# Gate statistics moved into the next image's gate, and the last stores of a group spread out

## The chip, the cores and the metric

The kernel runs on one core of one Trainium2 chip. The metric is the device time of the whole program in microseconds (us), the median of several executions. The core's engines are TensorE (PE), VectorE (DVE), ScalarE (ACT), GpSimd (POOL) and SyncE (SP), which here only issues transfers (DMAs). Each engine works through its own list of instructions in order; semaphores tie the lists together.

## The reference

The input x has 32 images of 8 channels of 256 x 256 numbers. Two layers follow one another, each added to its input; ahead of each stands a group normalisation over pairs of channels. Cut to what matters here:

```python
# layer 0, on the normalised x
grid = drive = x
for _ in range(15):                                   # the lattice
    mapped = 3.9 * grid * (1 - grid)
    physics = 0.7 * mapped + 0.3 * conv3x3_depthwise(mapped)
    grid = 0.85 * physics + 0.15 * drive
cml = clip(grid, 0.0001, 0.9999)
nca = sigmoid(conv1x1(relu(conv3x3(x, 8 -> 128)), 128 -> 8))
gin = concatenate([x, cml, nca])                      # 24 channels
g = sigmoid(conv1x1(relu(conv3x3(gin, 24 -> 8)), 8 -> 8))
y = x_in + g * cml + (1 - g) * nca
# layer 1: y normalised per image and pair of channels, quantised with
# sx = 127 / max(abs(normalised y)) over ALL images, 3x3 convolution
out = y + conv3x3(round(norm(y) * sx), round(w * sw)) / (sx * sw) + bias
```

So layer 1 needs, for each image, mean and variance of y (mean_y and rstd_y in the kernel), and the largest deviation over all images (dev_y), before it can start.

## The kernel before

**Two phases.** The first (up to about 13670 us) computes y for all 32 images and keeps it in scratch memory (y_s). The second quantises y, convolves it and writes the result. The change touches the first phase only.

**Four kinds of work in the first phase**, in groups of four images (GB = 4, NG = 8 groups):

- *prep* (normalise, L288): loads x, takes its statistics, writes normalised copies to scratch (xp_s, xq_s).
- *lattice* (L376): 8 channels of 15 steps for the four images of a group, as two streams of two images. A step goes over three tiles; for each tile and stream PE does matmuls (L486), DVE adds the drive (L494) and forms the next state (L499). Every second step neighbouring rows are exchanged by DMAs from m_a to m_a (exchange, L446). After the last step of a channel the result goes to scratch (cm_s) in 44 stores (store, L414).
- *nca* (L553): the hidden convolution (L563), the 1x1 convolution (L580), stores to nc_s.
- *gate* (L708): for each image ten iterations p over pairs of row blocks. An iteration loads nb from nc_s, cq from cm_s and xb from x (stage, L663, one iteration ahead), does three sets of convolution matmuls (L755, on xnb, cmb and nb), and then finishes the iteration before it (finish, L715: the 1x1 matmuls pg, sigmoid, mixing on POOL and DVE, bn_stats, maximum and minimum of the rows, a store to y_s).

**At an image's end** the gate forms the image's statistics from the rows' (L782 to L817): bn_aggr gives ma and mb, two matmuls add them up over the partitions (total, L785), DVE forms e from the mean, two more matmuls add up e, then come rstd_y and dev_y.

**Order of work.** PE's list is in the order in which the program is written out (manual_schedule, for PE alone); the lists of the other engines are put in order by a scheduler. The order of writing comes from generators: each `yield` gives the cost, in estimated us of PE, of what was written since the last. `together` (L823) writes a lattice step (5.91) and then as much filler as keeps filler and lattice in proportion; `both` (L837) mixes two fillers in proportion. While the lattice of group g is written, the filler is nca of group g, gate of group g-1 and prep of group g+1. For the last group the gates come alone, after everything else (L875).

**Background transfers.** The stores of a channel and the loads of the next channel's drive go into a list, `later`. After every lattice tile three of them are issued (background, L442). Only the last tile of a group's last channel issues all that is left at once, since the gate of that group, whose loads read cm_s, is written from the next lattice step on, and the store of a tensor has to be written out before the load that reads it.

Of the kernel before, what the change touches and what calls it, by code (L numbers as in the profile page):

```python
# [31 lines left out]
F32 = mybir.dt.float32  # L32
# [81 lines left out]
def kernel(  # L114
# [142 lines left out]
    with ExitStack() as one:  # L257
# [118 lines left out]
        def lattice(g):  # L376
# [65 lines left out]
            def background(n):  # L442
                for _ in range(min(n, len(later))):
                    nc.sync.dma_start(*later.pop(0))

            def exchange(t, k):  # L446

# [11 lines left out]
            for c in range(C):  # L459
                u = g * C + c  # L460
                ds = units[u]
                for step in range(STEPS):
                    if step == 7 and u + 1 < NG * C:
                        units[u + 1], dmas = load(u + 1)
                        later.extend(dmas)
                    if step == STEPS - 1:
                        background(len(later))
                    for i, ts in enumerate(tiles):

                        jobs = []  # L470
                        for s in range(2):
                            a2b = (step + s) % 2 == 0
                            n = NJ + 1 if a2b else NJ
                            pt = ps_c.tile([P, 512], F32, name="pt", tag="pt")
                            jobs.append((s, a2b, n, pt[:, : 6 * n].rearrange("p (t j) -> p t j", j=n)))

                        for part in range(3):
                            for s, a2b, n, pt in jobs:  # L480
                                own = m_a[s][:, ts, 1 : 2 + NJ] if a2b else m_b[s][:, ts, 0:NJ]
                                beside = m_a[s][:, ts, 0 : 1 + NJ] if a2b else m_b[s][:, ts, 1 : 1 + NJ]
                                low = a2b == (part != 1)
                                half = slice(0, 64) if low else slice(64, P)
                                k = 2 if part == 2 else 0 if a2b else 1
                                T.matmul(  # L486
                                    pt[half], lw[:, c, k, half], beside if part == 2 else own,
                                    start=part < 2, stop=part > 0,
                                )
                        for s, a2b, n, pt in jobs:  # L490
                            gt = gp.tile([P, 6 * (NJ + 1)], F32, name="gt", tag="gt")
                            gt = gt[:, : 6 * n].rearrange("p (t j) -> p t j", j=n)
                            d = ds[s][1 if a2b else 0]
                            V.scalar_tensor_tensor(gt, pt, FLOOR, d[:, ts, :], ALU.max, ALU.add)  # L494
                            if step == STEPS - 1:
                                V.tensor_scalar(d[:, ts, :], gt, 0.0001, 1.0 - 0.0001, ALU.max, ALU.min)
                                continue
                            to = m_b[s][:, ts, :] if a2b else m_a[s][:, ts, 1 : 1 + NJ]
                            V.scalar_tensor_tensor(to, gt, 1.0, gt, ALU.subtract, ALU.mult)  # L499
                            if a2b:  # L500

                                edge = m_b[s][:, ts, 0 : NJ + 1 : NJ]
                                G.tensor_tensor(  # L503
                                    edge, edge, junk.unsqueeze(1).to_broadcast([P, 6, 2]), ALU.mult
                                )
                        for s, a2b, n, pt in jobs:
                            for k in range(2):
                                if i != k + 1:
                                    continue
                                if step == STEPS - 1:  # L510
                                    b = g * GB + 2 * s + k
                                    later.extend(store(b, c, "b" if a2b else "a", ds[s][1 if a2b else 0], k))
                                elif not a2b:
                                    exchange(m_a[s], k)
                        if step == STEPS - 1 and u + 1 in units:
                            begin(units[u + 1], ts)

                        background(len(later) if (c, step, i) == (C - 1, STEPS - 1, 2) else 3)
                    yield 5.91

        ROWS = ((2, 4, 10, 12, 3, 5, 11, 13), (1, 6, 8, 14, 7, 9))
        FIRST, LAST = (2, 4, 10, 12), (1, 7, 9, 14)
# [185 lines left out]
        def gate(b):  # L708
# [37 lines left out]
            for p in range(10):  # L746
                n = 2 if p < 9 else 1
                xnb, xb, cmb, nb = ahead
                pa = ps_a.tile([P, 512], F32, name="pa", tag="acc")
                three = pa[:, : n * W].rearrange("p (k w) -> p k w", w=W)  # L750
                i = 0
                for s, t in ((0, xnb), (1, cmb), (2, nb)):
                    for dx in range(3):
                        for half in (slice(0, 64), slice(64, P)):
                            T.matmul(  # L755
                                three[half], gw[:, s * 3 + dx, half], t[:, :n, dx : dx + W],
                                start=(i == 0), stop=(i == 8),
                            )
                        i += 1
                    if s == 0 and p < 9:  # L760
                        ahead = stage(b, p + 1, sc)
                    elif s == 0 and (b + 1) % GB:
                        staged[b + 1] = begin_gate(b + 1)
                    if s < 2:
                        yield 2.6
                r1 = wk.tile([P, 512], F32, name="r1", tag="r1")
                S.activation(r1[:, : n * W], pa[:, : n * W], AF.Relu, bias=bv[:, 0:1])  # L767
                if last:
                    if done:
                        nc.sync.dma_start(*done)  # L770
                    done = finish(*last)
                yield 3.5
                last = (p, r1, xb, cmb, nb)
            if done:
# [2 lines left out]
            yield 0.9  # L777


            ma = st.tile([P, 2], F32, name="ma", tag="ma")  # L780
            mb = st.tile([P, 2], F32, name="mb", tag="mb")
            V.bn_aggr(ma, st_a.rearrange("p k s -> p (k s)"))  # L782
            V.bn_aggr(mb, st_b)

            def total(a, c):  # L785
                pm = ps_c.tile([P, 512], F32, name="pm", tag="pt")
# [1 line left out]
                T.matmul(pm[:, 0:1], sel_b, c, start=False, stop=True)  # L788
                return pm[:, 0:1]

            m, rstd = mean_y[:, b : b + 1], rstd_y[:, b : b + 1]
            yield 0.5
            V.tensor_copy(m, total(ma[:, 0:1], mb[:, 0:1]))
            e = st.tile([P, 2], F32, name="e2", tag="e2")
            for i, t in enumerate((ma, mb)):
                V.tensor_tensor(e[:, i : i + 1], t[:, 0:1], m, ALU.subtract)
                V.tensor_tensor(e[:, i : i + 1], e[:, i : i + 1], e[:, i : i + 1], ALU.mult)
                V.tensor_tensor(e[:, i : i + 1], e[:, i : i + 1], t[:, 1:2], ALU.add)
            yield 0.5
            V.tensor_scalar(rstd, total(e[:, 0:1], e[:, 1:2]), GN_EPS, None, ALU.add)  # L800
            G.tensor_tensor(rstd, rstd, mhalf[:, 0:1], ALU.pow)
            d = st.tile([P, 6], F32, name="dv", tag="dv")
            V.tensor_reduce(d[:, 0:1], mx[:, 0:9], AX.X, ALU.max)
            V.tensor_reduce(d[:, 1:2], mn[:, 0:9], AX.X, ALU.min)
            V.tensor_copy(d[:, 2:3], mx[:, 9:10])
            V.tensor_copy(d[:, 3:4], mn[:, 9:10])
            V.tensor_scalar(d[:, 0:4], d[:, 0:4], m, None, ALU.subtract)
            for i in range(2):
                V.tensor_scalar(
                    d[:, 2 * i + 1 : 2 * i + 2], d[:, 2 * i + 1 : 2 * i + 2], -1.0, None, ALU.mult  # L810
                )
                V.tensor_tensor(
                    d[:, 4 + i : 5 + i], d[:, 2 * i : 2 * i + 1], d[:, 2 * i + 1 : 2 * i + 2], ALU.max
                )
                V.tensor_tensor(d[:, 4 + i : 5 + i], d[:, 4 + i : 5 + i], masks[:, i : i + 1], ALU.mult)
            V.tensor_tensor(d[:, 4:5], d[:, 4:5], d[:, 5:6], ALU.max)
            V.tensor_tensor(dev_y[:, b : b + 1], d[:, 4:5], rstd, ALU.mult)  # L817

        def chain(*gens):
            for gen in gens:  # L820
# [38 lines left out]
            for b in range(g * GB, g * GB + GB):  # L859
                yield from f(b)  # L860

        units, later = {}, []
        T_NCA, T_GATE, T_PREP, T_LATTICE = 520.0, 340.0, 34.0, 8 * 45 * 1.97
        for _ in prep(0, (0,)):
            pass
        for g in range(NG):
            fill, t = images(nca, g), T_NCA
            if g:
                fill, t = both(fill, t, images(gate, g - 1), T_GATE), t + T_GATE
            if g + 1 < NG:  # L870
                fill, t = both(fill, t, prep(g + 1, (0, 1)), T_PREP), t + T_PREP
            if g == 0:
# [1 line left out]
            together(lattice(g), T_LATTICE, fill, t)  # L874
        for _ in images(gate, NG - 1):  # L875
            pass


    with ExitStack() as two:
# [110 lines left out]
```

## Time and profile before

| | |
|---|---|
| median of 3 runs | 14468.11 us (14463.03 to 14472.73) |
| profiled execution, span | 14446.0 us |
| mean granted TensorE clock | 0.959 |
| instructions | 229162 |
| groups | group 0 up to about 1670 us, then seven of some 1650 us; gates alone from 13257 to 13670 us; second phase to the end |

The page gives busy time for each engine. A row of a wait table names the engine and line that waited, the tile, what ended the wait, total us, number of waits and the longest. A timeline row has start, length, engine, line, operation, shapes, count, and in brackets how long the engine had been idle before it and what ended that. A row of a table by stretches gives, for a stretch of time, its length, the busy us of PE, PE's weight loads, DVE, ACT and POOL (with counts), the granted clock of TensorE (1.00 is full), the share of the DMA engines and GB/s. A float32 matmul counts as two passes, hence even counts.

### The profile page before, as it was taken

Reading aid. Unit: us, or ns where it says so; the run is one execution under the profiler, and the core shown is the slowest. Engines: PE = TensorE matmul, PEld = TensorE weight load, DVE = VectorE, ACT = ScalarE, POOL = GpSimd, SP = SyncE. Lnnn points to the kernel's source line nnn. Section 1 sums busy time; section 2 is a strip of 40 time slices with the busy share of each in tenths; the row PEclk is TensorE's granted clock in tenths of the full one; section 3 lists DMA queues with packets and bytes.
Section 4 is the critical chain, followed back from the end, with each engine's and each line's share of the span. In section 5 each row is a group of like instructions: output and inputs, shape, how many; then the busy total and the mean of one; then the engine's idle time right before and its main releaser. Section 6 shows DMA issues by size and latency. Waiting matters only on the chain.

```text
span 14446.0 us, 229162 instructions
## 1 busy us (share of the span) xinstructions
PE 13241.2 (92%) x81728; PEld 6420.6 (44%) x81728; DVE 8161.7 (56%) x16290; ACT 4043.5 (28%) x6274; POOL 2458.8 (17%) x4266
## 2 busy tenths in 40 slices
PE   2999999999999999999999999999999999999733
PEld 1554444444444444444444444444444444444211
DVE  3555555555555555555555555555555555555576
ACT  1333223232322232222223222322232222222122
POOL 1110111111111111111111111111111111112300
PEclk9999999999999999999999999999999999999866
DMA  5444444444444444444344434444444433333365
GB/s 149 93 101 93 92 99 105 101 95 104 105 97 101 106 98 98 101 100 111 88 101 105 108 91 102 103 108 94 97 104 108 95 84 80 86 75 79 114 195 176
DMA packets 2259557, 1496.71 MB, mean 104 GB/s; under 512 B 1061248, under 2 KB 2229504, under 8 KB 2258304
## 3 DMA queue, kind: packets, MB, share of 16 engines
q1 hardware_dynamic: 2176976, 1401.95, 41.1%
q10 hardware_dynamic: 81456, 80.12, 1.7%
q8 instruction: 663, 10.86, 0.3%
q14 instruction: 462, 3.78, 0.1%
HBM read 866.48 MB, written 478.69 MB: 93 GB/s over the span
## 4 chain that ended last, share of the span: by engine, by line
PE 76%; DVE 7%; DMA 7%; SPq 4%; issue 3%; ACT 1%; POOL 1%; ACTq 1%; POOLq 0%; DVEq 0%
PE pt L486 34%; PE ph L563 19%; PE pa L755 13%; PE acc L580 7%; DVE gt L494 2%; PE pg L721 1%; DMA im<-xp_s 1%; DMA out_dram<-ob 1%; SPq L941 1%; PE pt L934 1%; DVE m_b L499 1%; DMA yb<-y_s 1%; DMA m_a<-m_a 1%; DMA xb<-in_x_dram 1%; DMA xr<-in_x_dram 1%
## 5 line engine op out<-in xcount | busy, mean ns | idle before, releaser
L486 PE MATMUL pt<-m_a,lw 128*64 128x390 f32 x17280 | 5857.6, 497 | 160.4 <-DMA m_a<-m_a 121.4
L486 PE MATMUL pt<-m_b,lw 128*64 128x384 f32 x17280 | 5825.7, 492 | 23.0 <-DVE m_b L410 17.8
L573 ACT ACTIVATE h<-ph,bp_sb 128x512 f32<-128x512 f32 x4096 | 2584.7, 685 | 6258.0 <-PE ph L563 6187.8
L486 PEld LDWEIGHTS pt<-m_a,lw 128*64 128x64 f32 x17280 | 2312.1, 138 | 1824.9 <-issue 1670.8
L486 PEld LDWEIGHTS pt<-m_b,lw 128*64 128x64 f32 x17280 | 2316.1, 138 | 1601.4 <-issue 1465.6
L563 PE MATMUL ph<-im,wp_hi 48*128 48x512 f32 x12288 | 2713.5, 416 | 104.8 <-DMA im<-xp_s 54.4
L494 DVE SCALAR_TENSOR_TENSOR gt<-pt,d_b 128x390 f32<-128x390 f32 x2880 | 1610.6, 559 | 1828.2 <-PE pt L486 1824.9
L494 DVE SCALAR_TENSOR_TENSOR gt<-pt,d_a 128x384 f32<-128x384 f32 x2880 | 1584.9, 550 | 1826.9 <-PE pt L486 1826.5
L563 PE MATMUL ph<-im,wp_lo 48*128 48x512 f32 x12288 | 2598.5, 399 | 0.0
L503 POOL TENSOR_TENSOR m_b<-m_b,junk 128x12 f32<-128x12 f32 x2688 | 809.2, 301 | 8089.7 <-DVE m_b L499 7597.8
L563 PEld LDWEIGHTS ph<-im,wp_hi 48*128 48x128 f32 x12288 | 1331.4, 188 | 1013.5 <-DVE m_b L499 197.8
L499 DVE SCALAR_TENSOR_TENSOR m_b<-gt 128x390 f32<-128x390 f32 x2688 | 1562.5, 581 | 42.5 <-DVE gt L494 0.9
L499 DVE SCALAR_TENSOR_TENSOR m_a<-gt 128x384 f32<-128x384 f32 x2688 | 1525.9, 568 | 15.6
L563 PEld LDWEIGHTS ph<-im,wp_lo 48*128 48x128 f32 x12288 | 1327.1, 188 | 215.2
L580 PE MATMUL acc<-h,wu_z 128*32 128x512 f32 x8320 | 1170.7, 605 | 12.9 <-ACT h L573 7.3
L755 PE MATMUL pa<-xnb,gw 128*64 128x512 f32 (+1 forms) x3840 | 890.5, 596 | 0.2
L755 PE MATMUL pa<-cmb,gw 128*64 128x512 f32 (+1 forms) x3840 | 852.0, 576 | 10.0 <-POOL cmb L677 10.0
L755 PE MATMUL pa<-nb,gw 128*64 128x512 f32 (+1 forms) x3840 | 849.5, 574 | 0.0
L726 POOL TENSOR_TENSOR d<-cmb,nb 128x512 f32<-128x512 f32 x320 | 511.4, 1598 | 1608.5 <-DVE gate L730 1449.6
L730 DVE TENSOR_TENSOR gate<-gate,d 128x512 f32<-128x512 f32 x320 | 216.0, 675 | 870.3 <-ACT gate L723 856.3
L934 PE MATMUL pt<-qt,qw 128*128 128x512 bf16 (+1 forms) x960 | 269.2, 451 | 477.9 <-ACT ob L935 427.1
L767 ACT ACTIVATE r<-pa,bv 128x512 f32<-128x512 f32 x320 | 213.1, 666 | 1651.3 <-PE pa L755 1650.3
(132 smaller groups left out, 6966.1 us busy)
## 6 DMA issues: line engine op xcount, KB each, us to landing
im<-xp_s SPq DMA_DIRECT2D x1152, 193.5 KB
im<-xp_s SPq DMA_DIRECT2D x1216, 96.8 KB
d_a<-xq_s SPq DMA_DIRECT2D x2048, 36.0 KB
nb<-nc_s SPq DMA_DIRECT2D x288, 256.0 KB
cq<-cm_s SPq DMA_DIRECT2D x288, 256.0 KB
yb<-y_s ACTq DMA_DIRECT2D x29, 2432.0 KB
xb<-in_x_dram SPq DMA_DIRECT2D x544, 128.0 KB
xp_s<-hi SPq DMA_DIRECT2D x256, 258.0 KB
```

The lines of the kernel that those rows point to most:

```text
L486: T.matmul(pt[half], lw[:, c, k, half], beside if part == 2 else own, start=part < 2, stop=part > 0,)
L494: V.scalar_tensor_tensor(gt, pt, FLOOR, d[:, ts, :], ALU.max, ALU.add)
L499: V.scalar_tensor_tensor(to, gt, 1.0, gt, ALU.subtract, ALU.mult)
L503: G.tensor_tensor(edge, edge, junk.unsqueeze(1).to_broadcast([P, 6, 2]), ALU.mult)
L563: T.matmul(ph[:, :n].rearrange("p (h w) -> p h w", w=W), w[64 * i : 64 * i + 48, dx, :], rhs[:, :, dx : dx + W], start=(dx == 0 and w is w ...
L573: S.activation(h[:, :n], ph[:, :n], AF.Relu, bias=bp_sb)
L580: T.matmul(acc[32 * g : 32 * g + 32, :cols], wu_z[:, 24 - 8 * i : 56 - 8 * i], h, start=first, stop=last,)
L726: G.tensor_tensor(three(d), cmb[:, :n, 1 : 1 + W], nin, ALU.subtract)
L730: V.tensor_tensor(y[:, :cols], gt[:, :cols], d[:, :cols], ALU.mult)
L755: T.matmul(three[half], gw[:, s * 3 + dx, half], t[:, :n, dx : dx + W], start=(i == 0), stop=(i == 8),)
L767: S.activation(r1[:, : n * W], pa[:, : n * W], AF.Relu, bias=bv[:, 0:1])
L934: T.matmul(pt, qw[:, dx, :], q[:, k0 : k0 + n, dx : dx + W], start=(dx == 0), stop=(dx == 2))
```

## The change

There are two edits.

**Statistics in pieces.** What the end of an image's gate did in one go becomes three functions, put into a list `sums`: gather (the two bn_aggr), means (the first two matmuls and e), deviations (the other two matmuls, rstd_y, dev_y). Each iteration of the following image's gate takes one from the list, after finish of the iteration before; the last image's are run after the last gate. The two yields of 0.5 between the pieces go. The aim is that matmuls which need a result of DVE are not written directly behind the work that they wait for.

**The last stores of a group.** The burst goes, and the stores left over from a group's last channel are issued three after each tile in the first steps of the next group's lattice. A counter `issued` counts what was issued from the list, `stored[g]` is its value at which all stores of group g are out, and `after` holds back the gate of group g until then, handing out empty units of 4.0. The last group, with no lattice after it, still issues all at once. The aim is that SyncE is not taken up by a burst while the next group's lattice begins.

```diff
             def background(n):
                 for _ in range(min(n, len(later))):
                     nc.sync.dma_start(*later.pop(0))
+                    issued[0] += 1
...
-                        background(len(later) if (c, step, i) == (C - 1, STEPS - 1, 2) else 3)
+                        background(3)
                     yield 5.91
+
+            stored[g] = issued[0] + len(later)
+            if g == NG - 1:
+                background(len(later))
...
                     done = finish(*last)
+                if sums:
+                    sums.pop(0)()
                 yield 3.5
...
-            V.bn_aggr(ma, st_a.rearrange("p k s -> p (k s)"))
-            V.bn_aggr(mb, st_b)
...
-            yield 0.5
-            V.tensor_copy(m, total(ma[:, 0:1], mb[:, 0:1]))
...
-            yield 0.5
-            V.tensor_scalar(rstd, total(e[:, 0:1], e[:, 1:2]), GN_EPS, None, ALU.add)
...
+            def gather():
+                V.bn_aggr(ma, st_a.rearrange("p k s -> p (k s)"))
+                V.bn_aggr(mb, st_b)
+
+            def means():
+                V.tensor_copy(m, total(ma[:, 0:1], mb[:, 0:1]))
...
+            def deviations():
+                V.tensor_scalar(rstd, total(e[:, 0:1], e[:, 1:2]), GN_EPS, None, ALU.add)
...
+            sums.extend((gather, means, deviations))
...
+        def after(g, gen):
+
+            while issued[0] < stored[g]:
+                yield 4.0
+            yield from gen
...
             if g:
-                fill, t = both(fill, t, images(gate, g - 1), T_GATE), t + T_GATE
+                fill, t = both(fill, t, after(g - 1, images(gate, g - 1)), T_GATE), t + T_GATE
...
         for _ in images(gate, NG - 1):
             pass
+        while sums:
+            sums.pop(0)()
```

More of the change, by code (lines that the diff above doesn't have):

```diff
@@ L781, in gate @@
             mb = st.tile([P, 2], F32, name="mb", tag="mb")
-            V.bn_aggr(ma, st_a.rearrange("p k s -> p (k s)"))
-            V.bn_aggr(mb, st_b)
+            e = st.tile([P, 2], F32, name="e2", tag="e2")
+            m, rstd = mean_y[:, b : b + 1], rstd_y[:, b : b + 1]
             def total(a, c):
@@ L789, in total @@
                 return pm[:, 0:1]
-            m, rstd = mean_y[:, b : b + 1], rstd_y[:, b : b + 1]
-            yield 0.5
-            V.tensor_copy(m, total(ma[:, 0:1], mb[:, 0:1]))
[L794 to L798, printed above, removed]
@@ L799, in gate @@
-            yield 0.5
-            V.tensor_scalar(rstd, total(e[:, 0:1], e[:, 1:2]), GN_EPS, None, ALU.add)
[L801 to L816, printed above, removed]
@@ L817, in gate @@
-            V.tensor_tensor(dev_y[:, b : b + 1], d[:, 4:5], rstd, ALU.mult)
+            def gather():
[3 more added lines that the diff above has]
+                V.tensor_copy(m, total(ma[:, 0:1], mb[:, 0:1]))
+                for i, t in enumerate((ma, mb)):
+                    V.tensor_tensor(e[:, i : i + 1], t[:, 0:1], m, ALU.subtract)
+                    V.tensor_tensor(e[:, i : i + 1], e[:, i : i + 1], e[:, i : i + 1], ALU.mult)
+                    V.tensor_tensor(e[:, i : i + 1], e[:, i : i + 1], t[:, 1:2], ALU.add)
@@ new lines, in deviations @@
+            def deviations():
+                V.tensor_scalar(rstd, total(e[:, 0:1], e[:, 1:2]), GN_EPS, None, ALU.add)
+                G.tensor_tensor(rstd, rstd, mhalf[:, 0:1], ALU.pow)
+                d = st.tile([P, 6], F32, name="dv", tag="dv")
+                V.tensor_reduce(d[:, 0:1], mx[:, 0:9], AX.X, ALU.max)
+                V.tensor_reduce(d[:, 1:2], mn[:, 0:9], AX.X, ALU.min)
+                V.tensor_copy(d[:, 2:3], mx[:, 9:10])
+                V.tensor_copy(d[:, 3:4], mn[:, 9:10])
+                V.tensor_scalar(d[:, 0:4], d[:, 0:4], m, None, ALU.subtract)
+                for i in range(2):
+                    lo_, hi_ = d[:, 2 * i + 1 : 2 * i + 2], d[:, 2 * i : 2 * i + 1]
+                    V.tensor_scalar(lo_, lo_, -1.0, None, ALU.mult)
+                    V.tensor_tensor(d[:, 4 + i : 5 + i], hi_, lo_, ALU.max)
+                    V.tensor_tensor(
+                        d[:, 4 + i : 5 + i], d[:, 4 + i : 5 + i], masks[:, i : i + 1], ALU.mult
+                    )
+                V.tensor_tensor(d[:, 4:5], d[:, 4:5], d[:, 5:6], ALU.max)
+                V.tensor_tensor(dev_y[:, b : b + 1], d[:, 4:5], rstd, ALU.mult)
@@ L860, in images @@
                 yield from f(b)
-        units, later = {}, []
+        units, later, issued, stored, sums = {}, [], [0], {}, []
+        def after(g, gen):
+            while issued[0] < stored[g]:
+                yield 4.0
+            yield from gen
         T_NCA, T_GATE, T_PREP, T_LATTICE = 520.0, 340.0, 34.0, 8 * 45 * 1.97
```

## The prediction

> **What bounds the kernel now.** I read the page first (engine shares, the 40 slices), then TensorE's waits by line, then its timeline at one image's end, then stretches of time side by side.
>
> ```profile
> PE 13241.2 (92%) x81728; PEld 6420.6 (44%) x81728; DVE 8161.7 (56%) x16290; ACT 4043.5 (28%) x6274; POOL 2458.8 (17%) x4266
> ```
>
> PE's waits, the statistics with the largest other one (total us, times, longest):
>
> ```profile
> PE pt L486 <- DMA m_a<-m_a: 121.4, 41, 10.1
> PE pm L788 <- DVE dv L805: 88.4, 20, 4.6
> PE pm L787 <- DVE ma L782: 78.0, 11, 11.4
> PE pm L787 <- DVE dv L812: 23.5, 21, 1.5
> PE pm L788 <- DVE mb L783: 7.6, 12, 3.4
> PE pm L787 <- DVE e L798: 4.2, 4, 1.1
> ```
>
> TensorE (PE) bounds everything up to about 13670 us; the last 770 us (the second convolution, L934) are not touched. Five of the six are waits of four tiny 128x1 matmuls, the statistics of a finished gate image (L787, L788): 88.4 + 78.0 + 23.5 + 7.6 + 4.2 = 201.7 us. By stretches, 150.1 us of them lie between 1500 and 13257 us, in 27 images (5.6 us each), the rest in the tail, where only gates run. PE executes in program order, so lattice and NCA matmuls stand behind these four. One image's end in the interior, then one in the tail (start, length, idle before):
>
> ```profile
> 2109.49 0.38 PE L787 MATMUL pm<-ma,sel_a 128*128 128x1 f32 x2
> 2114.43 0.59 PE L788 MATMUL pm<-mb,sel_b 128*128 128x1 f32 x2 [4.56 <-DVE dv L805]
> 2116.03 0.56 PE L787 MATMUL pm<-e,sel_a 128*128 128x1 f32 x2 [1.01 <-DVE dv L812]
> 2116.94 4.58 PE L755 MATMUL pa<-xnb,gw 128*64 128x512 f32 x12
> ...
> 13364.58 1.46 PE L721 MATMUL pg<-r,gw 128*64 128x512 f32 x8
> 13377.44 0.58 PE L787 MATMUL pm<-ma,sel_a 128*128 128x1 f32 x2 [11.41 <-DVE ma L782]
> 13381.09 4.50 PE L755 MATMUL pa<-xnb,gw 128*64 128x512 f32 x12
> 13385.43 2.74 PE L755 MATMUL pa<-cmb,gw 128*64 128x512 f32 x12
> ```
>
> Twelve gate passes take 2.74 us normally, but 4.58 and 4.50 right after the pause: a pause costs another 1.8 us. The stretches (PE busy, PEld, DVE, ACT, POOL, then granted clock) say the same:
>
> ```profile
> 2100.00:2150.00 50.00, 44.43 (x271) 21.16 (x270) 26.05 (x69) 10.55 (x18) 6.24 (x14) 0.93 0.32 78
> 2150.00:2200.00 50.00, 50.00 (x326) 23.32 (x322) 28.33 (x59) 13.42 (x21) 8.46 (x16) 1.00 0.41 87
> ...
> 700.00:1500.00 800.00, 759.68 (x4954) 399.16 (x4952) 442.72 (x914) 256.33 (x402) 82.01 (x204) 0.96 0.44 97
> 3380.00:3740.00 360.00, 358.71 (x2268) 168.95 (x2266) 204.37 (x416) 107.04 (x164) 65.50 (x114) 1.00 0.41 100
> ```
>
> The first row holds an image's end, the second none. The third is group 0, which has no gate to fill with; the fourth has lattice, NCA and gate and no image's end: PE is full at full clock there.
>
> **What the Trainium skill says.** "TensorE: Matmul & The Clock Gate", section "What's actually happening": after an idle window of about 3.4 us the array runs at half clock until it has been busy for about as long. The trace agrees: 4.50 to 4.58 against 2.74 us, clock 0.93 in that stretch. "Perfetto Trace Analysis", section "Sequencer Loop": an engine takes its instructions in turn and each waits for its semaphore; the 4.56 us above, with ready matmuls behind, fits. "DMA: Bandwidth & Descriptors", section "Issuing engines are not separate DMA queues", calls the issue time "usually small relative to the DMA itself"; here SyncE took 4.81 us to issue ten cm_s stores at 4986.82, so 41 cost some 20 us.
>
> **The change, part by part.**
>
> *Statistics.* No operation is added or taken away: four matmuls, 23 small DVE operations (0.12 to 0.39 us each) and one POOL power per image, as before. They move into iterations p = 0, 1 and 2 of the next image's gate. In the interior an image lasts 436 us (2109.5 to 2545.9), so an iteration is some 44 us, and bn_aggr ends long before PE reaches the matmuls that read it. In the tail an iteration is 8.6 us: bn_aggr of mb ended 12 us after the last pg (13575.2 against 13563.2), and the matmul now comes after two iterations, 16 us. So PE's wait goes in both. The new wait of DVE for these matmuls (L793, L800) was there before, at 0.4 to 0.8 us, and DVE is at 56%. Interior gain: 150.1 us of idle plus 27 x 1.8 us of slow clock = 199 us. I keep 189, since a pause also lets DVE and the DMAs catch up and some of it should come back as other waits; the two 50 us rows speak for little.
>
> *Tail.* Three images' ends, 13366.0 to 13381.1 = 15 us each, plus 1.8 slow, less 1.1 us of statistics matmuls that only move. But the next image's iteration 1 needs xnb, whose second half was normalised only at 13576.0 (the last of the ends), and PE would want it at 13571. I take 5 us of that, with its clock, as left: 9 to 16 each, taken as 11: 33 us. The last image's statistics still run bare at the end, as before.
>
> *Stores.* A channel's last step makes 44 cm_s stores (two streams, two images each, 10 or 12 by format). At a group's end 41 of them went in one burst; now they go three after each lattice tile like any channel's, so 38 are left over, 9 a step: all are out after five steps of the next group. Behind the burst on SyncE stand the exchanges of m_a. At the first boundary this shows: PE waits 10.07 us for m_a at 1699.57, and the burst ran from 1671 to 1697. With the clock, 12 us gained. At the six others PE has no wait after the burst: the 7.2 to 8.2 us for m_a come before it (4978.42 against a burst from 4983.89), where DVE had stood 5.2 us before a bn_stats for an xr load. I count nothing there.
>
> *The gate's wait.* It can't start before step 5; meanwhile it hands out units of 4.0 that hold no work. Its share is 340/894 of 7.45 units a step, 2.8, so three such units pass, 12. Two yields of 0.5 less per image give back 4. So 8 units, about one iteration, run after the lattice: no loss, since gates alone keep PE at 8.6 us an iteration. But four to five steps have only lattice and NCA, as in group 0: from 700 to 1500 us PE idles 40 us and loses 4% of clock (30 us), in 66 steps of 12.1 us, so 1.06 us a step, against about 0.05 in the fourth row. 1.0 x 4.3 steps x 7 boundaries = 30 us lost. At the last boundary PE waits for cm_s to come back (10.0 us for cmb until 13284.72); the leftover iteration now fills 7 us of that.
>
> *Sum.* -189 - 33 - 12 - 7 + 30 = -211 us: 14468 - 211 = **14257**.
>
> **Rivals.** *The waits come back*: PE reaches xnb, the lattice's DVE results or im earlier and waits there. For it: the waits on L494 (44.5 us) and im (54.4) exist already. Against it: 1.3 us of idle in 360. With half of the gain returned, 14468 - 106 = 14362. *The boundary changes as well*: with the gate shifted, the 7.5 us waits for m_a, with their 1.8 us of clock, go at six boundaries, 56 us more: 14201. Against it: their cause, the xr load, is not touched. *The head of each group starves*: stores among the exchanges plus no gate, as in the ragged end of group 0, where 1600 to 1700 us had 77.6 us of busy PE at clock 0.89: about a third lost, 4 us a step. To be slower it must be more than twice that: with 10 us a step, the one wait seen, 301 us are lost instead of 30, 14468 - 241 + 301 = 14528. Against it: stores at three a tile ran beside the lattice in seven of eight channels.
>
> **How the numbers follow.** Forecast 0.64, waits come back 0.19, boundary better 0.12, starved 0.05. The range takes in the tail at 16 each (15 us lower), the whole 199 and the better boundary at the low end: 14198; at the high end it reaches into the first rival, 14350. Outside: starved, about half of the first rival, a few per cent below. Faster 0.94, same 0.02, slower 0.04 (a mild starvation may only cancel the gain).
>
> **What would show it.** The waits of L787 and L788 (new lines) nearly gone; clock 1.00 where an image ends; in the tail, images about 87 us apart instead of 98.5; no ten cm_s issues in a row at the seven inner boundaries; some PE idle in the first five steps of each group. Wrong, if PE's waits on L486, L563 or L755 grow by over 60 us, or the heads of groups show clock under 0.9.

## The result and the profile after

| | before | after |
|---|---|---|
| median (lowest to highest) | 14466.45 us (14463.03 to 14472.73) | 14417.28 us (14383.04 to 14422.08) |
| ratio, 95% interval | | 0.9960 (0.9943 to 0.9978) |
| profiled span | 14446.0 us | 14414.7 us |
| mean granted TensorE clock | 0.959 | 0.963 |

The change brings 49 us, 0.4%, where 211 were forecast; the time lies above the range. The shares of the engines have hardly moved (the page's first part, after):

```profile
PE 13267.4 (92%) x81728; PEld 6423.3 (45%) x81728; DVE 8213.1 (57%) x16290; ACT 4039.8 (28%) x6274; POOL 2445.9 (17%) x4266
```

Yet what was to go did go. Two of TensorE's waits before that matter here (total us, times, longest):

```profile
PE ph L563 <- DMA im<-xp_s: 54.4, 24, 16.2
PE ph L563 <- DVE gt L494: 44.5, 71, 3.6
```

and its waits after:

```profile
PE pt L487 <- DMA m_a<-m_a: 122.4, 74, 6.5
PE ph L567 <- DVE gt L495: 113.1, 151, 4.0
PE pa L759 <- DVE xnb L700: 43.5, 9, 7.1
PE pa L759 <- POOL cmb L681: 17.4, 1, 17.4
PE ph L567 <- ACT gate L727: 16.9, 6, 3.5
PE pt L487 <- ACT h L577: 14.7, 7, 3.1
PE pm L794 <- DVE ma L799: 5.2, 1, 5.2
```

Of the 201.7 us of waits for statistics only those of the last image are left (5.2 us here, 6.5 with its two short ones). But waits of the hidden convolution for a PSUM buffer that DVE empties (L567 on gt) have grown from 44.5 to 113.1 us, pt for h from 1.2 to 14.7, and two rows are new: the gate for xnb 43.5 and ph for the gate's sigmoid 16.9. The waits of 7 to 10 us for m_a are gone (longest 6.5), their sum is not: 74 short ones instead of 41.

An image's end in the interior and one in the tail, on PE's timeline:

```profile
5565.25 1.03 PE L725 MATMUL pg<-r,gw 128*64 128x512 f32 x4
5566.21 0.38 PE L794 MATMUL pm<-ma,sel_a 128*128 128x1 f32 x2
5566.46 0.36 PE L795 MATMUL pm<-mb,sel_b 128*128 128x1 f32 x2
5566.75 0.54 PE L487 MATMUL pt<-m_b,lw 128*64 128x384 f32 x1
...
13374.14 4.20 PE L759 MATMUL pa<-xnb,gw 128*64 128x512 f32 x12 [3.80 <-DVE xnb L700]
13384.28 0.38 PE L794 MATMUL pm<-ma,sel_a 128*128 128x1 f32 x2
13384.52 0.36 PE L795 MATMUL pm<-mb,sel_b 128*128 128x1 f32 x2
```

No idle bracket on the statistics and a lattice matmul straight behind them. So the question is where some 160 us went. Counting the lattice matmuls in the trace gives the length of each group (us; "start" is up to the end of group 0):

| | start | 1 | 2 | 3 | 4 | 5 | 6 | 7 | gates alone |
|---|---|---|---|---|---|---|---|---|---|
| before | 1673.9 | 1671.5 | 1653.9 | 1659.0 | 1662.6 | 1653.2 | 1659.2 | 1624.3 | 413.1 |
| after | 1681.1 | 1648.1 | 1668.3 | 1665.8 | 1672.0 | 1662.2 | 1655.9 | 1597.3 | 389.0 |

Groups 1 and 7 and the tail gain 23, 27 and 24 us. The five groups between, each with four images whose pauses have gone, are 7 us *longer* on average (1664.8 against 1657.6). Inside them the saving has been paid back completely.

### The profile page after: what moved, and what is told of

It reads as the page before. It is cut to its first block, busy times and chain, and to the rows that moved or that the text cites. A ratio compares the mean times of both kernels' runs of the same rounds, so it can differ in the third digit from the quotient of the medians.

```text
span 14414.7 us, 229163 instructions
## 1 busy us (share of the span) xinstructions
PE 13267.4 (92%) x81728; PEld 6423.3 (45%) x81728; DVE 8213.1 (57%) x16290; ACT 4039.8 (28%) x6274; POOL 2445.9 (17%) x4266
## 4 chain that ended last, share of the span: by engine, by line
PE 70%; DMA 9%; DVE 9%; SPq 5%; issue 3%; POOL 2%; ACT 1%; ACTq 1%; POOLq 0%; DVEq 0%
PE pt L487 31%; PE ph L567 18%; PE pa L759 13%; PE acc L584 7%; DVE gt L495 2%; DMA im<-xp_s 1%; PE pg L725 1%; DMA xp_s<-lo 1%; SPq L545 1%; DVE m_b L500 1%; DMA xb<-in_x_dram 1%; DMA m_a<-m_a 1%; DMA out_dram<-ob 1%; SPq L960 1%; PE pt L953 1%
## 5 line engine op out<-in xcount | busy, mean ns | idle before, releaser
L567 PE MATMUL ph<-im,wp_hi 48*128 48x512 f32 x12288 | 2800.2, 419 | 174.2 <-DVE gt L495 113.1
L567 PE MATMUL ph<-im,wp_lo 48*128 48x512 f32 x12288 | 2675.2, 402 | 0.0
L495 DVE SCALAR_TENSOR_TENSOR gt<-pt,d_b 128x390 f32<-128x390 f32 x2880 | 1605.3, 557 | 1714.7 <-PE pt L487 1711.2
L495 DVE SCALAR_TENSOR_TENSOR gt<-pt,d_a 128x384 f32<-128x384 f32 x2880 | 1580.3, 549 | 1694.5 <-PE pt L487 1694.1
L567 PEld LDWEIGHTS ph<-im,wp_hi 48*128 48x128 f32 x12288 | 1417.5, 189 | 1081.7 <-DVE gt L495 303.9
L500 DVE SCALAR_TENSOR_TENSOR m_b<-gt 128x390 f32<-128x390 f32 x2688 | 1546.1, 575 | 44.5 <-DVE gt L495 2.3
L567 PEld LDWEIGHTS ph<-im,wp_lo 48*128 48x128 f32 x12288 | 1417.0, 189 | 217.3
L759 PE MATMUL pa<-xnb,gw 128*64 128x512 f32 (+1 forms) x3840 | 879.9, 588 | 43.7 <-DVE xnb L700 43.5
L759 PE MATMUL pa<-cmb,gw 128*64 128x512 f32 (+1 forms) x3840 | 857.6, 577 | 17.4 <-POOL cmb L681 17.4
L700 DVE TENSOR_SCALAR xnb<-xb,sc 128x256 f32<-128x256 f32 x608 | 290.7, 493 | 796.7 <-DMA xb<-in_x_dram 759.5
```

Of the source, the lines that this page charges most:

```text
L567: T.matmul(ph[:, :n].rearrange("p (h w) -> p h w", w=W), w[64 * i : 64 * i + 48, dx, :], rhs[:, :, dx : dx + W], start=(dx == 0 and w is w ...
L700: V.tensor_scalar(xnb[:, k, 1 : 1 + W], xb[:, k, :], sc[:, i : i + 1], sc[:, 1:2], ALU.subtract, ALU.mult,)
L759: T.matmul(three[half], gw[:, s * 3 + dx, half], t[:, :n, dx : dx + W], start=(i == 0), stop=(i == 8),)
```

## The experiments

The expectations name theories by letters. **A**: VectorE stands in its list ahead of work that PE needs; in the first experiments that means the wait for the statistics' sums, from the constant tile on the wait for something late, the xb load above all. **B**: the pieces bring the forecast 200 us and the later gate eats 150. **C**: many small limits hold PE, and what one pause frees is absorbed at the next. **D**: the wait for xb is where VectorE blocks the lattice. Later, within B, **E**: the gate's later start does it, and **F**: the stores among the exchanges do it. Every ratio is to the kernel before, on the same chip, with its 95% interval.

**Each half alone.** The first kernel takes the statistics apart and keeps the burst; the second keeps the statistics at the image's end and spreads the stores. The first against the change (the second is the change with the statistics written as before):

```diff
-                        background(3)
+                        background(len(later) if (c, step, i) == (C - 1, STEPS - 1, 2) else 3)
...
-                fill, t = both(fill, t, after(g - 1, images(gate, g - 1)), T_GATE), t + T_GATE
+                fill, t = both(fill, t, images(gate, g - 1), T_GATE), t + T_GATE
```

> The statistics in pieces alone; a group's last stores go in one burst and its gate starts at once, as before. Theory A (the wait has moved: VectorE now stands at the two instructions that read the sums out of PSUM, until TensorE reaches the matmuls, 179 us in seven groups against 31 before, and the lattice's work stands behind it): the boundary matters little, 14400 to 14440 us. Theory B (the statistics bring about 200 us, as I forecast, and the later start of the gate eats 150 of them): about 14260 us.

> The other half alone: stores three after each tile and the gate held back; the statistics at the image's end as before. Theory A: within 25 us of the kernel before, 14440 to 14490. Theory B: about 150 us slower, 14610.

Statistics alone: 14262.74 us, 0.9863 (0.9850 to 0.9877), 200 us faster than before's 14463.23. Stores alone: 14397.14 us, 0.9954 (0.9940 to 0.9967), 66 us faster. Each half gains, and together they gain no more than the smaller one: the loss is neither half's own but comes of the two together. B's number for the first kernel was right, and its sign for the second was wrong; A, as it was meant here, missed both. The same 1660 us of two kernels (length, PE, PEld, DVE, ACT and POOL busy, clock, DMA share, GB/s), after:

```profile
4990.00:6650.00 1660.00, 1617.99 (x10065) 786.66 (x10062) 952.22 (x1989) 476.33 (x742) 305.90 (x528) 0.98 0.44 100
```

and statistics alone:

```profile
4990.00:6650.00 1660.00, 1634.06 (x10255) 782.62 (x10249) 973.13 (x2030) 482.96 (x753) 314.04 (x538) 0.99 0.44 103
```

190 matmul instructions more pass in the same stretch, 1.9%. DVE's waits between 1690 and 13250 us say what it stands for; before:

```profile
DVE xnb L696 <- DMA xb<-in_x_dram: 457.7, 148, 10.3
DVE hi L342 <- DMA xp_s<-hi: 78.1, 24, 7.4
DVE rstd_y L800 <- PE pm L788: 16.6, 20, 0.8
DVE mean_y L793 <- PE pm L788: 14.4, 27, 0.6
```

after:

```profile
DVE xnb L700 <- DMA xb<-in_x_dram: 624.3, 222, 9.9
DVE hi L342 <- DMA xp_s<-hi: 132.2, 36, 9.5
DVE mean_y L803 <- PE pm L795: 107.3, 27, 7.0
DVE rstd_y L810 <- PE pm L795: 71.7, 21, 5.7
```

and statistics alone:

```profile
DVE xnb L696 <- DMA xb<-in_x_dram: 387.4, 149, 8.5
DVE hi L342 <- DMA xp_s<-hi: 67.9, 29, 4.9
DVE mean_y L799 <- PE pm L791: 82.8, 29, 5.9
```

Two suspects, then: the wait for the statistics' matmuls, which the change itself makes (107.3 + 71.7 us, where before it was 14.4 + 16.6; with statistics alone it is 82.8 + 41.1), and the wait for xb.

**The two suspects, first try.** One kernel computes the two matmul sums and doesn't read them; the other writes the normalisation of xb at the end of its iteration.

```diff
-                V.tensor_copy(m, total(ma[:, 0:1], mb[:, 0:1]))
+                total(ma[:, 0:1], mb[:, 0:1])
+                V.tensor_copy(m, ma[:, 0:1])
...
-                V.tensor_scalar(rstd, total(e[:, 0:1], e[:, 1:2]), GN_EPS, None, ALU.add)
+                total(e[:, 0:1], e[:, 1:2])
+                V.tensor_scalar(rstd, ma[:, 1:2], GN_EPS, None, ALU.add)
```

> The changed kernel, but VectorE takes mean and variance from the partition's own ma and not from the matmuls' sums, which are still computed and read by nobody (the sum over the partitions is left out of the statistics). Same matmuls, same number of VectorE instructions, only the two waits of VectorE for TensorE go. Theory A: those 179 us of VectorE waits vanish, TensorE's waits for the lattice's evacuations (94 us for a ph buffer in seven groups) go back to some 30, 14300 to 14350 us. Theory C (TensorE is simply held by many small limits, and what one pause frees is absorbed at the next): within 25 us of the changed kernel, 14390 to 14440.

> The changed kernel with the normalisation of xb written at the end of the gate's iteration and not right behind its load. VectorE waits 624 us for xb in seven groups (458 before). Theory D (this is where VectorE blocks the lattice): that wait falls under 200 us and the time to about 14330 us. Theory A: the xb wait falls but the lattice gains little, 14390 to 14430.

Sums unread: 14371.36 us, 0.9940 (0.9927 to 0.9952), 109 us above statistics alone, between A's range and C's: the sums are at most a minor part of the loss. Normalisation late: 14388.02 us, 0.9948 (0.9935 to 0.9960), but it decides nothing on D, since DVE's wait for xb stayed at 621.1 us (624.3 in the change). DVE's list is put in order by the scheduler; writing the operation later didn't shorten the stand that it was meant to shorten.

**The gate's start or the stores.** From the change, ten more stores go out after each tile of the first step, so that no empty unit is needed and the gate starts at once; and from statistics alone (burst kept), three empty units ahead of each gate. Both pieces of code are shown against the change; the second kernel also keeps the burst, as above.

```diff
-                        background(3)
+                        background(13 if g and c == step == 0 else 3)
```

```diff
-            while issued[0] < stored[g]:
+            for _ in range(3):
                 yield 4.0
```

> The changed kernel, but the 38 left-over stores go 13 after each tile of the next group's first step, so that the gate is written from that step's filler on: no empty unit. Theory E (what costs, beside the pieces, is the gate's later start: three empty units shift it against lattice and prep): about as the pieces alone, 14250 to 14300 us. Theory F (the stores among the next group's exchanges cost): 14350 or more.

> The statistics in pieces with the burst of stores as before, and the gate held back by three empty units of 4.0 all the same. Theory E: as the changed kernel, 14380 to 14430 us. Theory F: as the pieces alone, 14250 to 14290.

Without the shift: 14215.94 us, 0.9852 (0.9837 to 0.9867). With the shift and no spread: 14356.69 us, 0.9948 (0.9935 to 0.9960). So this shift of the gate brings the loss about, with the stores spread or in a burst, and without it there is none. E holds, though the times are 34 and 23 us under its ranges (the kernel before, too, was 25 us faster here than beside the first four kernels); F falls.

**What the shift does: xb.** After three empty units the gate's iterations fall elsewhere between lattice and prep. One spot of the change, DVE's timeline:

```profile
2693.41 0.21 DVE L306 BATCH_NORM_AGGREGATE mv<-stats 128x2 f32<-128x12 f32 x1
2702.51 0.93 DVE L700 TENSOR_SCALAR xnb<-xb,sc 128x256 f32<-128x256 f32 x2 [8.89 <-DMA xb<-in_x_dram]
2703.35 0.56 DVE L495 SCALAR_TENSOR_TENSOR gt<-pt,d_b 128x390 f32<-128x390 f32 x1
2703.82 0.55 DVE L495 SCALAR_TENSOR_TENSOR gt<-pt,d_a 128x384 f32<-128x384 f32 x1
```

SyncE's, with start and issue time:

```profile
2690.63 0.57 SPq L450 DMA_DIRECT2D m_a<-m_a  x1
2691.24 0.56 SPq L451 DMA_DIRECT2D m_a<-m_a  x1
2691.84 0.44 SPq L774 DMA_DIRECT2D y_s<-gate  x1
2692.39 0.40 SPq L671 DMA_DIRECT2D nb<-nc_s  x1
2692.84 0.49 SPq L676 DMA_DIRECT2D cq<-cm_s  x1
2693.43 1.87 SPq L545 DMA_DIRECT2D im<-xp_s  x4
2695.34 1.27 SPq L690 DMA_DIRECT2D xb<-in_x_dram  x2
```

and PE's:

```profile
2713.97 0.50 PE L567 MATMUL ph<-im,wp_hi 48*128 48x512 f32 x1
2717.16 0.79 PE L567 MATMUL ph<-im,wp_hi 48*128 48x512 f32 x1 [2.69 <-DVE gt L495]
```

DVE is free at 2693.6 us; next on its list is xnb. The load that it needs is issued 1.7 us later, behind exchanges, a store, nb, cq and four im loads, and ends DVE's wait at 2702.5. The lattice's additions (L495) stand behind xnb on DVE's list; PE has run lattice matmuls since 2697.4, and DVE starts on their results at 2703.35. From there it has hardly a gap, and it is still behind when PE, at 2714, needs a PSUM buffer. The worst form is the start of a group's gate, the first xnb of which has no earlier iteration to be loaded in. There is one such wait in each of the five middle groups, 30.2 us together:

```profile
5064.51 4.99 PE L759 MATMUL pa<-xnb,gw 128*64 128x512 f32 x12 [5.72 <-DVE xnb L700]
```

5.72 us of idle, then 4.99 us for twelve passes that take 2.74 at full clock. To test it, xnb is made from a constant tile in place of xb (xfix, a view of weights that are already there), then also with the sums unread:

```diff
-                    xnb[:, k, 1 : 1 + W], xb[:, k, :], sc[:, i : i + 1], sc[:, 1:2],
+                    xnb[:, k, 1 : 1 + W], xfix[:, k, :], sc[:, i : i + 1], sc[:, 1:2],
```

> The changed kernel, but VectorE normalises a constant tile in place of xb (the gate's convolution doesn't see x; xb is still loaded, and GpSimd still reads it). Same instructions, only VectorE's wait for the load of xb goes: 624 us in seven groups of the changed kernel, against 387 where the pieces are alone. Theory A (VectorE stands in its list before something late, the lattice stands behind it, and about half of that reaches TensorE): 14150 to 14280 us. Theory C (TensorE is held by many small limits): 14390 to 14430.

> The changed kernel with both of VectorE's waits away: xnb from a constant tile, and mean and variance not from the matmuls' sums (left out: x in the gate's convolution, the sum over the partitions). Theory A: some 40 us below the kernel with xnb from a constant tile, 14100 to 14240. Theory C: as with the sums unread alone, 14350 to 14390.

14200.47 us, 0.9843 (0.9830 to 0.9857), and with both 14216.07 us, 0.9852 (0.9839 to 0.9866). With DVE's wait for the xb load gone the loss is gone; the sums add nothing to that, where 40 us were expected. DVE doesn't stop standing at xnb, though. In the first of these kernels it waits there for PE to be done with xnb's buffer:

```profile
DVE xnb L700 <- PE pa L760: 469.1, 184, 21.7
```

Such a wait ends with PE's own progress. The waits of 5 us and more at xnb, whatever ended them, add up to 332 us in the change, 194 with statistics alone and 180 here (1690 to 13250 us).

**The load first, nothing left out.** The xb load is written ahead of nb and cq in stage: in the change, in the kernel with the stores in the first step, and in the kernel before.

```diff
+            xb = bp2.tile([P, 2, W], F32, name="xb", tag="xb", bufs=3)
...
+                nc.sync.dma_start(
+                    xb[r0 * C : r1_ * C, k, :],
...
-            xb = bp2.tile([P, 2, W], F32, name="xb", tag="xb", bufs=3)
...
-                nc.sync.dma_start(
-                    xb[r0 * C : r1_ * C, k, :],
```

> The changed kernel with the load of xb written ahead of those of nb and cq in each iteration; nothing is left out. Theory A (VectorE's standing before late xb loads is what takes the gain back): VectorE's wait for xb falls from 624 to under 450 us in seven groups, ratio to the kernel before 0.986 to 0.991. If the wait falls and the ratio stays at 0.994 to 0.997, the wait is a symptom.

> The stores in the first step (no empty unit), and the load of xb first. Theory A: VectorE's wait for xb falls below the 408 us of the stores in the first step alone; ratio 0.980 to 0.985, the fastest so far. If xb is no longer what limits there, 0.985 to 0.987.

> The kernel before, with the load of xb written first, nothing else. If the gain of 1.0% that this edit brought in the changed kernel is a gain of its own, 0.989 to 0.992. If it mostly undoes what the shifted gate did to VectorE's list (Theory A), as little as in the kernel with the stores in the first step, 0.996 to 1.000.

In the change: 14219.10 us, 0.9858 (0.9843 to 0.9874): back at the level of statistics alone. In the kernel without the shift: 14180.17 us, 0.9823 (0.9810 to 0.9837), another 0.3%. In the kernel before: 14428.19 us, 1.0001 (0.9993 to 1.0009), nothing. This speaks for it that most of what the edit gains in the change is not its own: it undoes what the shift did. DVE's row for it in the change with the load first misses the size expected:

```profile
DVE xnb L700 <- DMA xb<-in_x_dram: 546.2, 238, 12.5
```

Only 78 us less than the 624.3 of after, with more waits (238). The total is a poor measure. Taken one by one from DVE's timeline, the long ones are (waits of 5 us and more for xb, 1690 to 13270 us):

| kernel | waits | us | ratio |
|---|---|---|---|
| change | 51 | 329 | 0.9960 |
| change, sums unread | 46 | 309 | 0.9940 |
| change, normalisation late | 42 | 292 | 0.9948 |
| statistics alone, three empty units | 48 | 339 | 0.9948 |
| statistics alone, one empty unit | 70 | 540 | 0.9950 |
| statistics alone | 24 | 151 | 0.9863 |
| change, stores in the first step | 25 | 158 | 0.9852 |
| change, load first | 30 | 184 | 0.9858 |
| statistics alone, six empty units | 30 | 182 | 0.9838 |
| stores in the first step, load first | 14 | 83 | 0.9823 |
| six empty units, load first | 15 | 112 | 0.9802 |
| before | 41 | 267 | 1 |
| before, load first | 27 | 172 | 1.0001 |
| stores alone | 30 | 224 | 0.9954 |

The eleven kernels with the statistics in pieces fall into two sets: 292 us or more with a ratio of at least 0.9940, and 184 or less with at most 0.9863. The limit of 5 us was chosen with the times known; limits from 2 to 7 us part the same two sets, and so, narrowly, does the total (546 us and less against 595 and more). Within a set the sum doesn't rank them (540 us cost no more than 339). In the last three, which keep the pauses, it says nothing: before loses 95 us of long waits with the load first, and gains nothing.

What makes a wait long is that the load goes out late. Of the 6.45 us that the 51 long waits of the change last on average, 3.0 pass before SyncE has issued the load; of the 1.75 us of the 172 shorter ones it is 0.3. From the start of the issue to the end of the wait it is 4.1 us in both.

How much of PE's waiting leads back to xb can be counted too. From every wait of PE for a tile of DVE's (gt, xnb, m_a or m_b, 1690 to 13250 us) one goes back along DVE's instructions to its last gap of over 1 us and notes what ended that gap. In the change 65 of 134 us lead to xb, with statistics alone 27 of 70: over half of what is new. With three empty units and the burst it is 34 of 109, and with one unit only 7 of 127; there the gate's sigmoid (55), prep's stores (31) and prep's loads (21) take its place. So in the change xb is the largest single source. For one empty unit the sum of the long waits goes along with the loss but doesn't explain it.

**How much of a shift.** One and six empty units instead of three, and six with the load first.

> The same with one empty unit. If each unit costs the same: 0.989. If it is how the iterations fall: not between 0.988 and 0.990, but near one of the two ends, or beyond.

> The statistics in pieces, the burst of stores, and six empty units of 4.0 ahead of each group's gate (three gave a ratio of 0.9948, none 0.9863). If each empty unit costs (less to fill with, more left over): about 1.003. If it is how the gate's iterations fall against lattice and prep, the ratio is not a line in the number of units: anything from 0.985 to 0.997.

> Statistics in pieces, burst, six empty units (0.9838) and the load of xb first. Theory A: a little better, as without a shift, 0.980 to 0.983. If the order of the lists alone decides, whatever made them: anything up to 0.995.

One unit: 14362.92 us, 0.9950 (0.9938 to 0.9963). Six: 14195.92 us, 0.9838 (0.9824 to 0.9851). None was 0.9863 and three 0.9948. There is no price per unit: one costs as much as three, and six cost less than none. What counts is where the iterations land among lattice steps and prep. Six units with the load first is the fastest kernel of the study: 14143.15 us, 0.9802 (0.9789 to 0.9816), 284 us below the before of its run.

## Why the prediction was wrong

**The step that failed** is the sum itself, with the sentence that feeds it, "I keep 189, since a pause also lets DVE and the DMAs catch up and some of it should come back as other waits". Ten us were kept back for that. Statistics alone gain about what the prediction's first two terms say, 200 us against 222, but that agreement is in part luck: the waits for m_a at six boundaries, 7.2 to 8.2 us each, which the prediction left out, went in that kernel too, and its middle groups are only 20.6 us shorter, where 189 us in seven groups make 27. And the terms don't add: with the stores' half the gain falls to 49, although that half alone gains 66. I priced the empty units at PE's idle in the steps without a gate and took the gate, once started, to be the same gate at another time. Its xnb, on DVE's list, and its loads, on SyncE's, landed elsewhere among lattice and prep, and DVE stood 329 us in long waits for xb instead of the 151 of statistics alone.

How this makes up the time can be checked in the five middle groups. PE's idle plus the time lost to a slow clock, counted from the trace, is 42.1 + 26.6 = 68.7 us a group after, and 27.0 + 13.7 = 40.7 with statistics alone. The difference is 28.0; the groups last 1664.8 and 1637.0 us, 27.8 apart. Idle and clock are all of it. Against before (43.6 + 29.7 = 73.3 us, 1657.6 long) the sum doesn't close as well: 4.6 us less lost and 7.2 longer, so 12 us lie within what the trace calls busy. Weight loads waiting for gt, 157.5 us before and 271.2 after between 1690 and 13250 us, would be large enough, but they fall to 213.5 with statistics alone, where the same 12 us a group are in excess. So they are not the whole of it, and what the rest is stays open.

**The rival that came closest** is "the waits come back", on the rows it named: gt rose from 44.5 to 113.1 us. It was wrong in size (three quarters came back, not half), im fell (54.4 to 39.8), and it took the waits for what the missing pauses do by themselves; with the pieces by themselves gt rose only to 66.7, and 200 us were gained. The warning written down, waits on L486, L563 or L755 growing by over 60 us, is what happened: gt alone by 69.

**Point by point.**

- *Waits of the statistics nearly gone*: right, 201.7 to 6.5 us.
- *Tail*: 27 us instead of 33. PE's timeline shows 88, 91 and 89 us between the means' matmuls of neighbouring images, where 98.5 stood before and 87 was forecast. (The 24 us of the table by groups also hold the wait for cmb, below, that grew by 7.4.) The xnb wait left over was taken as 5 us "with its clock"; it measured 3.80, 1.00, 4.86 and 3.69, three of them followed by passes of 4.2 to 4.95 us instead of 2.74, which is another 1.5 to 2.2 each.
- *First boundary*: the 10.07 us wait is gone (longest there now 3.2), as forecast.
- *Six inner boundaries, "I count nothing there"*: wrong. The 7.2 to 8.2 us waits for m_a vanished in the change and in each half alone, which was the second rival's point. Their cause as the prediction has it, an xr load, wasn't touched, but DVE's waits for xr shrank (116.6 to 44.3 us, longest 7.0 to 3.7): it fell elsewhere on the lists. This made the boundaries better; the groups as a whole are longer all the same.
- *Last boundary*: 7 us forecast, from a wait for cmb which the leftover iteration would fill. That wait grew instead, from 10.0 to 17.4 us. But the last group became 27 us shorter, and with the stores alone 36, about 13 of them in PE's idle and 12 in the clock. I didn't take it further.
- *Head of each group*: right in kind. The 60 us from 4997 us on, after, and the same stretch from 4999 us on, before:

```profile
4997.00:5057.00 60.00, 54.89 (x331) 29.73 (x332) 36.07 (x78) 13.12 (x21) 6.34 (x17) 0.91 0.19 38
```

```profile
4999.00:5059.00 60.00, 60.00 (x364) 30.32 (x366) 30.22 (x67) 12.78 (x20) 10.88 (x23) 0.95 0.36 86
```

  That is 5.1 us of idle and 0.04 x 60 = 2.4 us of clock, 7.5 against the 4.3 of the prediction. It isn't what the 160 us hang on: six empty units hold the gate back for longer, and that kernel is among the fastest.
- *Stores*: spread as forecast. At the same boundary SyncE issues at most six cm_s stores in a row, where 44 stood in a row; 14 are still between two pairs of exchanges (4977.4 to 5008.3 us). Stores alone made the kernel faster.
- *The range*: its low end, 14198, is above what the three parts named for it make, 15 + 10 + 56 us below 14257, which is 14176. Nothing hangs on it here.

**What the lists of two engines decide.** The Trainium skill, "Perfetto Trace Analysis", section "Sequencer Loop", says that an instruction waits for its semaphore at its place in its engine's list. The prediction used this for PE alone. The trace agrees for DVE as well: it stood 8.89 us from 2693.6 on, while PE ran lattice matmuls from 2697.4, and the load's own place on SyncE's list decided much of how long. The Trainium skill, "DMA: Bandwidth & Descriptors", section "Issuing engines are not separate DMA queues", calls the issue time usually small beside the transfer. One issue agrees with that, 0.4 to 0.65 us here; nine in a row don't: from 2690.63 on they took 4.7 us before the xb load's turn came, and from its own issue to the end of DVE's wait it was 7.2 (2695.34 to 2702.51).

**What stays open.** That long waits cost nothing as long as the pauses are there fits a DVE which catches up in the pause at each image's end; this is argued, no run isolates it. A reordered load also changes the lists of DVE and SyncE around it, so that its full effect can't be put down to the wait of xnb alone; taking the wait for the load away by the constant gives the same time (0.9843 against 0.9858), which speaks for the wait, but that edit changes the lists too. That any other order of the lists would do as well is made less likely, not ruled out, by the two edits that left the wait long (sums unread, normalisation late) and gained little. Why one empty unit lands badly and six well would need the scheduler's lists compared iteration by iteration.

## What to carry to other kernels

When PE's pauses are taken out of a kernel in which several engines work through fixed lists, don't price the pause alone: look for an engine that stands in its list for a load while results that PE needs stand behind it, and write that load ahead of those whose users come later. A shift of one stream of work against another can change every engine's list, and its effect need not add to that of another edit; measure each half alone, and try several shifts, since here 0, 1, 3 and 6 units gave 0.9863, 0.9950, 0.9948 and 0.9838. Look at long waits beside the total: 546 us, mostly in short pieces, gave the same ratio as 387. And follow PE's waits back along the other engine's list before a row of the wait table is called the cause.

## What the runs showed that was not expected

- Two edits that gain 200 and 66 us alone gain 49 together.
- The order of three loads is worth 1.0% in one version (0.9960 to 0.9858), 0.3 and 0.4% in two others (0.9852 to 0.9823, 0.9838 to 0.9802) and nothing in the kernel before.
- A wait for xb was long because the load was issued late, not because it then took longer: 4.1 us on average from issue to the end of the wait, for the long waits and for the short ones. The one shown above is an exception, with 5.9 us after the issue of its second part (2696.61 to 2702.51).
- PE's busy share says little: 92% before and after, 93% in the fastest kernel. The granted clock tells more: 0.959 before, 0.963 after, 0.966 to 0.969 in the fast versions.
